# Attention weights staged in sixteen tiles, the key/query ring set up in the first plan, and the last query part stores issued by ScalarE

## The chip, the core and the metric

One core of a Trainium2 chip runs the whole program. Its compute engines are TensorE (PE in the profile, with its weight loads as PEld), VectorE (DVE), ScalarE (ACT) and GpSimd (POOL); SyncE (SP) issues DMAs. Each engine has one queue of instructions and takes them in order. An instruction that waits for another engine holds back everything behind it on its own queue. The metric is the device time of one execution in microseconds (us); lower is better. A time and the span of the profiled execution differ by what lies around the first and the last instruction.

## The reference

The program computes one decoder layer for 32 batches of 128 positions and 512 features, in float32. Cut to what matters:

```python
x = layernorm(x + attn(x))          # 16 heads; sequence of 128; causal; rotary
x = layernorm(x + xattn(x, ctx))    # 8 heads; here features attend to features
x = layernorm(x + ffn(x))           # 512 -> 2048 -> 512, quantized

def xattn(q, c):                     # per batch (128, 512), seen as 8 heads of 16 rows
    s = einsum('hdq,hdl->hql', q, c) / sqrt(16)      # 512 x 512 scores per head
    return gamma * einsum('hql,hdl->hdq', softmax(s), c)

def ffn(x):
    h = gelu(silu(bitlinear(x, w1, b1)))
    h = layer_norm(h) * ln_g + ln_b
    return bitlinear(h, w2, b2)      # rms norm, rounding to 8 bit, ternary weights
```

The attention's weights Wq, Wk, Wv and Wo are float32 and stay so; the feed-forward weights are rounded to -1, 0, 1.

## The kernel before, in words

The kernel has two stages, one after the other, with all 32 batches in each.

**Stage 1** (to about 560 us) does the self-attention. The four weight matrices are loaded in sixteen pieces of 128 x 512 (`split_weight`, `part`, lines 311 to 321). Each piece is split into a high part, which ScalarE or VectorE casts (lines 317 and 315), and a low part, which VectorE subtracts (line 318). A projection is then twelve matmuls (`project`, line 346): high by high, low by high, high by low. The pieces pass through a staging tile `wst` with four buffers, so the fifth load waits until the first piece is split. `load` (line 332) fetches a batch of x twice, turned (`xt`) and plain (`xs`). `stage_q` makes the projections and the rotary products, `stage_s` the scores, the masked softmax and its transposes, `stage_o` the weighted sum, the output projection and the first layernorm. Its result x1 is stored to DRAM (line 521). `split3` cuts it into three bfloat16 parts in a tile `sp`, and stores six part copies of 128 KB to `q_d` (line 364, from SP). `context` does the same for the context into `k_d`, and stores the values to `c_d` (line 381). All PSUM tiles of stage 1 come from one group of eight banks.

**Stage 2** does cross-attention and the feed-forward part. For each batch and each half of the heads, a key tile `kp` and a query tile `qp` are loaded from `k_d` and `q_d` (six parts of 16 rows, 96 rows). They live in a ring of four pairs (`NQ`). `b1_` makes 16 products (line 677), of which VectorE takes row maxima (line 681); `shift` turns the maxima on TensorE (line 691), splits them in two (lines 694, 695), and SP stores them as rows 96 and 97 of `qp` (line 700). `b2_` can then make the shifted scores (line 756), ScalarE their exponentials (line 759), and TensorE the sum with the values `cT` (line 766), whose upper half is ones, so that the denominators come along. `final`, `up_`, `gelu_` and `down_` make the second layernorm and the feed-forward part.

**The hand-over.** The ring lies where the weights of q, k and v were. When the last projection matmul of q, k, v has been put into the program, `early` (line 578) opens the ring and issues twelve loads from SP: the ones rows (line 587) and, for all four pairs, keys and queries (line 589). The value tiles `cT` belong to a pool of stage 2 and are opened and set to one by GpSimd (line 616) behind all of stage 1; the first load into them is line 663. The sixteen products of the first half batch belong to stage 2's plan.

**What sets the order.** Everything is emitted by a list planner (`Plan`, line 83), once per stage. Operations are filed under a kind such as `SP.xs` or `PE.mx`; within a kind they keep their order. At each step the planner takes, of the heads of all kinds, the one that can start first by its own cost figures; starts are compared in steps of `slack` microseconds, and within one step the lower priority number goes first. The priority is the batch number plus a figure for the kind (`OFF1`, `OFF2`). `rel` keeps an operation from starting before a planned time. On each engine the order so found is the order of the program; at run time an engine waits for what the order demands.

## Time and profile before

| what | value |
|---|---|
| median of 3 runs | 1673.24 us (1671.13 to 1677.36) |
| the profiled execution's own time | 1675.28 us |
| its span | 1673.5 us |
| mean granted TensorE clock | 0.973 of full speed |
| busy share of the span: TensorE, VectorE, ScalarE, GpSimd | 93%, 83%, 86%, 75% |
| last projection matmul of q, k, v in stage 1 ends | 549.12 us |
| last output projection matmul ends | about 562.6 us |
| first shifted score of stage 2 | 585.55 us |

The page gives the span in 40 slices of about 42 us each with the busy share of every engine in tenths. The windows view gives the same for stretches of one's own choice: length, then busy time of each engine with the number of its instructions, then the granted TensorE clock, the busy share of the DMA engines and GB/s. The timeline lists instructions by start, with length, engine, line and operand names; for the DMA queues a merged row stands for several issues. The waits view lists who waited for whom: total us, times, longest.

### The profile page before, as it was taken

What the parts mean: (1) busy time and instruction counts of PE and PEld (TensorE: products, weight loads), DVE (VectorE), ACT (ScalarE), POOL (GpSimd) and SP (SyncE); (2) the same over time, 40 slices, a digit from 0 to 9 for tenths busy, and PEclk for the clock granted to TensorE, in tenths of its full rate; (3) what the DMA queues carried; (4) which work ended last, traced back from release to release, by engine and by line L of the source; (5) the groups of instructions that cost most, each with busy time, mean ns of one, the idle gap of its engine ahead of it and who ended that gap; (6) DMA issues with size and microseconds to landing.
All of it is one profiled execution on the core that took longest, in us unless ns stands there. A gap on an engine that the chain in (4) does not pass through costs nothing.

```text
span 1673.5 us, 30270 instructions
## 1 busy us (share of the span) xinstructions
PE 1551.4 (93%) x9540; PEld 785.0 (47%) x9540; DVE 1383.9 (83%) x3315; ACT 1432.7 (86%) x2950; POOL 1251.5 (75%) x1679
## 2 busy tenths in 40 slices
PE   6999999999999799999999999999999999999844
PEld 4878777777778333333333333333333333333211
DVE  6877776777777678899999989899899999998674
ACT  4889989899976367999989989899999999998963
POOL 3777778777787404679879888878978888986772
PEclk8999999999999799999999999999999999999977
DMA  6476677766664654355455345545544544544221
GB/s 226 163 236 232 226 231 244 255 233 214 209 208 153 185 177 122 93 129 145 113 133 147 105 129 139 131 115 139 142 110 128 153 110 134 149 122 123 69 62 50
DMA packets 235680, 258.71 MB, mean 155 GB/s; under 512 B 110072, under 2 KB 159224, under 8 KB 235136
## 3 DMA queue, kind: packets, MB, share of 16 engines
q1 hardware_dynamic: 235520, 256.78, 52.8%
q8 instruction: 75, 1.23, 0.3%
q14 instruction: 85, 0.70, 0.1%
HBM read 142.41 MB, written 92.81 MB: 141 GB/s over the span
## 4 chain that ended last, share of the span: by engine, by line
PE 41%; DVE 18%; POOL 16%; DMA 9%; ACT 8%; issue 7%; SPq 1%; POOLq 0%; ACTq 0%; DVEq 0%
PE banka L346 12%; DVE mt L681 8%; PE acc L766 7%; PE sT L756 6%; POOL z L972 6%; PE mx L677 5%; PE m L925 2%; DVE am L998 2%; PE banka L477 2%; DMA qd<-sp 2%; POOL z L794 2%; PE banka L447 2%; ACT pr L465 1%; ACT ex L759 1%; PE banka L496 1%
## 5 line engine op out<-in xcount | busy, mean ns | idle before, releaser
L681 DVE TENSOR_REDUCE mt<-mx 128x1 f32<-128x512 f32 x1024 | 643.4, 679 | 54.9 <-PE mx L677 52.9
L759 ACT ACTIVATE ex<-sT 128x512 f32<-128x512 f32 x1024 | 533.9, 615 | 77.9 <-PE sT L756 74.4
L677 PE MATMUL mx<-kp,qp 96*128 96x512 bf16 x1024 | 336.9, 386 | 21.5 <-DVE mt L681 17.7
L756 PE MATMUL sT<-qp,kp 98*128 98x512 bf16 x1024 | 320.7, 385 | 15.9 <-DMA qp<-mlo 13.3
L766 PE MATMUL acc<-ex,cT 128*32 128x512 f32 x2048 | 289.4, 637 | 0.0
L465 ACT ACTIVATE pr<-pr,nm 128x128 f32<-128x128 f32 x512 | 198.9, 394 | 4.1 <-DVE nm L459 4.1
L756 PEld LDWEIGHTS <-kp 98*128 98x128 bf16 x1024 | 90.3, 98 | 223.7 <-issue 125.1
L677 PEld LDWEIGHTS <-qp 96*128 96x128 bf16 x1024 | 96.3, 98 | 195.5 <-issue 95.1
L972 POOL TENSOR_TENSOR z<-z,bb_b 128x512 f32<-128x512 f32 x119 | 154.4, 1301 | 0.3
L972 POOL TENSOR_TENSOR z<-z,g_b 128x512 f32<-128x512 f32 x119 | 153.5, 1297 | 0.5
L459 DVE CUSTOM_DVE_ANT_0 pr<-banka,cmask 128x128 f32<-128x128 f32 x512 | 111.0, 286 | 35.9 <-PE banka L447 35.2
L1009 PE MATMUL m<-w2q,q2T 128*128 128x512 fp8e4 x464 | 116.7, 385 | 16.4 <-DMA q2T<-q 16.4
L766 PEld LDWEIGHTS acc<-ex,cT 128*32 128x32 f32 x2048 | 70.6, 184 | 114.1 <-issue 108.8
L925 PE MATMUL m<-w1q,q1T 128*128 128x512 fp8e4 x464 | 119.1, 378 | 2.7 <-DVE z L928 1.3
L1009 PEld LDWEIGHTS <-q2T 128*128 128x128 f16 x512 | 51.0, 101 | 104.5 <-DMA q2T<-q 34.9
L465 ACT ACTIVATION_READ_ACCUMULATOR pr<-pr,nm 128x1 f32 x512 | 98.0, 191 | 0.0
L794 POOL TENSOR_SCALAR z<-z,nmu,rs 128x512 f32<-128x512 f32 x119 | 94.5, 801 | 1.8
L361 POOL TENSOR_TENSOR sp<-spr,sp 128x512 bf16<-128x512 f32 x64 | 76.7, 1200 | 20.3 <-ACT sp L359 18.2
L928 DVE SCALAR_TENSOR_TENSOR z<-m,dq,b_b 128x512 f32<-128x512 f32 x116 | 85.0, 733 | 1.8 <-PE m L925 1.5
L925 PEld LDWEIGHTS <-q1T 128*128 128x128 f16 x512 | 49.2, 97 | 76.1 <-issue 19.9
L846 POOL TENSOR_TENSOR num<-num,rden 128x512 f32<-128x512 f32 x29 | 37.1, 1278 | 62.3 <-DMA rden<-rd 62.2
L346 PE MATMUL banka<-wqkh,xh 128*128 128x512 f32 x256 | 73.9, 411 | 10.3 <-ACT xh L388 10.3
(152 smaller groups left out, 3247.9 us busy)
## 6 DMA issues: line engine op xcount, KB each, us to landing
kd<-sp SPq DMA_DIRECT2D x192, 128.0 KB
qd<-sp SPq DMA_DIRECT2D x192, 128.0 KB
kp<-kd SPq DMA_DIRECT2D x64, 384.0 KB
qp<-qd SPq DMA_DIRECT2D x64, 384.0 KB
F<-f SPq DMA_DIRECT2D x64, 256.0 KB
xt<-in_xT SPq DMA_DIRECT2D x32, 256.0 KB
xs<-in_x SPq DMA_DIRECT2D x32, 256.0 KB
ct<-in_cxT SPq DMA_DIRECT2D x32, 256.0 KB
```

The lines of the kernel that those rows point to most:

```text
L346: nc.tensor.matmul(pq.t, parts[a].t[:, c, :], w[t][:, c, sl], start=k == 0, stop=k == 11)
L459: nc.vector.tensor_tensor_reduce(pr.t[:, c, :], sc.t[:, c * P:(c + 1) * P], cmask, -1.0, 3e38, ALU.add, ALU.min, nm.t[:, c:c + 1])
L465: nc.scalar.activation(pr.t[:, c, :], pr.t[:, c, :], AF.Exp, scale=-1.0, bias=nm.t[:, c:c + 1], accum_out=den.t[:, c:c + 1])
L677: nc.tensor.matmul(sc.t[:, j, :], q.t[0:NPR, h, (qc + j) * P:(qc + j + 1) * P], k.t[0:NPR, h, :], start=True, stop=True)
L681: pl.op("DVE.mx", 0.064 + 0.534 * W, lambda: nc.vector.tensor_reduce(mt.t[:, i:i + W], sc.t, AX.X, ALU.max), (sc,), (mt,), p, join=True)
L756: nc.tensor.matmul(sc.t[:, i, :], k.t[:, h, lc * P:(lc + 1) * P], q.t[:, h, :], start=True, stop=True)
L759: pl.op("ACT.ex", 0.052 + 0.426 * SW, lambda: nc.scalar.activation(ex.t[:, j:j + SW, :], sc.t, AF.Exp, scale=1.0 / XD ** 0.5), (sc,), (ex, ...
L766: nc.tensor.matmul(acc.t[32 * h:32 * h + 32, :], v.t[:, :, XH * lc + 4 * g + h], exs[h // 2].t[:, h % 2, :], start=lc == 0, stop=lc == NC - 1)
L794: pl.op(e + "." + p, cost + 0.1, lambda: en(e).tensor_scalar(o.t[:, sl], v.t[:, sl], sh.t, sc.t, ALU.add, ALU.mult), ins, outs, prio)
L925: nc.tensor.matmul(flat(pz)[:, i * 512:(i + 1) * 512], q1T.t[:, c, :], w1q[:, c, (n + i) * 512:(n + i + 1) * 512], start=c == 0, stop=c == ...
L972: pl.op(e + kind, 0.148 + 0.0021 * w if e == "Pool" else 0.05 + 0.00105 * w, lambda: en(e).tensor_tensor(t(), t(), other[:, sl], op), src, ...
L1009: nc.tensor.matmul(flat(py)[:, 0:D], q2T.t[:, c, :], w2q[:, c, :], start=c == 0, stop=c == NI - 1)
```

## The change

Six things are changed.

- **Weights.** The sixteen weight pieces are staged in sixteen different tiles: seven of tag `prT`, five of `pr` and four of `wst`, all of which stage 1 has anyway. No weight load waits for an earlier piece. The low part of six of the sixteen pieces is made by GpSimd. The load of the first `xt` gets priority -1000.
- **Ring.** The value tiles `cT` are opened and set to one in `early`, beside the ring. `early` issues only the ones rows; the eight key and query loads become planned operations of stage 1 (`SP.kq`), held back until the stores they read and the last q, k, v matmul.
- **Carry.** The products, maxima and shift of the first half batch (`b1_` for batch 0, half 0) are planned in stage 1, in two PSUM banks of its group (`mx=2`).
- **Stores.** The six query part stores of each of the last two batches are issued by ScalarE (`ACT.xsd`).
- **Planner.** `op` takes extra dependencies (`after`); a projection matmul counts 0.244 us instead of 0.236; stage 1's `slack` is 0.05 instead of 0.02.
- **Figures.** Every figure in `OFF1` and `OFF2` is another, so the order is another in both stages.

The functions `b1_`, `shift`, `last`, `slow`, `eng`, `bank` and `flat` move ahead of stage 1 with the same arithmetic. The diff, cut (of the configuration and the planner's figures only a few entries are shown):

```diff
-CFG = dict(..., early=5, ...)
+CFG = dict(..., carry=1, ...)
-OFF2 = {'SP.const': -264.67, 'x.kq': 390.3, 'SP.v': 77.29, 'PE.mx': -381.13, 'DVE.mx': 126.92, ...}
+OFF2 = {'SP.const': -363.47, 'x.kq': 222.35, 'SP.v': 14.78, 'PE.mx': -501.79, 'DVE.mx': 339.36, ...}
-OFF1 = {'SP.x': 76.47, 'SP.w': -83.56, 'ACT.w': 1251.46, 'DVE.wl': 97.39, ..., 'SP.xs': 975.4}
+OFF1 = {'SP.x': 75.59, 'SP.w': -99.74, 'ACT.w': 1071.41, 'DVE.wl': -171.32, ..., 'SP.xs': 1284.61,
+  'ACT.xsd': 162.58, 'SP.kq': 326.77, 'PE.mx': 327.89, 'DVE.mx': -118.6, 'PE.mT': 188.75, ...}
-C1 = dict(pace=15.0, ..., tr=3, sc=4, ..., slack=0.02)
+C1 = dict(late=2, pace=15.0, ..., tr=3, mx=2, sc=4, ..., slack=0.05)
...
+        stage = ["prT"] * C1["prT"] + ["pr"] * C1["pr"] + ["wst"] * C1["wst"]
...
                 def part(c, sl=sl, w=w):
-                    t = pl.buf("wst")
-                    dma("w", lambda: nc.sync.dma_start(t.t, src[:, c, sl]), 262, (), (t,), -1.0)
+                    tag = stage.pop(0)
+                    t = pl.buf(tag)
...
+                    dma("w", lambda: nc.sync.dma_start(flat_(), src[:, c, sl]), 262, (), (t,), -1.0)
...
-                    pl.op("DVE.wl", 0.6, lambda: nc.vector.tensor_tensor(
-                        lo[:, c, sl], t.t, hi[:, c, sl].bitcast(F32), ALU.subtract), (t,), (w,), -1.0)
+                    e = "Pool" if c == 3 or c == 1 and name != "wqk" else "DVE"
+                    pl.op(e + ".wl", 0.6 if e == "DVE" else 1.23, lambda: en(e).tensor_tensor(
+                        lo[:, c, sl], flat_(), hi[:, c, sl].bitcast(F32), ALU.subtract), (t,), (w,), -1.0)
...
-            dma("x", lambda: nc.sync.dma_start(xt.t, xT[b]), 262, (), (xt,), at, (b - 1.5) * C1["pace"])
+            dma("x", lambda: nc.sync.dma_start(xt.t, xT[b]), 262, (), (xt,), at if b else -1000.0, (b - 1.5) * C1["pace"])
...
-                pl.op("PE." + kind, 0.236 * m, mm, used + [wb], (pq,), prio)
+                pl.op("PE." + kind, 0.244 * m, mm, used + [wb], (pq,), prio)
...
             for s, k in enumerate(parts):
-                dma(kind, lambda s=s, k=k: nc.sync.dma_start(dst[s].rearrange("t h c -> h t c"), sp.t[:, k, :]), 131,
-                    (sp,), (), prio)
+                q = nc.scalar if late else nc.sync
+                pl.op("ACT.xsd" if late else "SP." + kind, 0.55, lambda s=s, k=k, q=q: q.dma_start(
+                    dst[s].rearrange("t h c -> h t c"), sp.t[:, k, :]), (sp,), (), prio, 2.6)
...
-            split3("xs", x1, q_d[b], Q_PARTS, at)
+            split3("xs", x1, q_d[b], Q_PARTS, at, b >= NB1 - C1['late'])
...
+        for i in range(NQ):
+            b, g = divmod(i, 2)
+            K[b, g], Q[b, g] = pl.buf("kp"), pl.buf("qp")
+            for t, d, kind in ((K[b, g], k_d, "cs"), (Q[b, g], q_d, "xs")):
+                dma("kq", lambda t=t, d=d, b=b, g=g: nc.sync.dma_start(
+                    t.t[0:NPR], d[b][:, :, 4 * g:4 * g + 4, :].rearrange("s t h c -> (s t) h c")), 393, (), (t,), NB1 + b + 0.5 * g,
+                    after=pl.kinds["SP." + kind][6 * b:6 * b + 6] + pl.kinds["PE.qkv"][-1:])
+            if i < CARRY:
+                b1_(b, g, NB1 + b + 0.5 * g)
...
             qk = pool(ctx, "qk", side="right")
+            for i in range(CFG["cT"]):
+                t = qk.tile([P, 2 * XD, NC * XH], F32, tag=f"cT{i}", name=f"cT{i}")
+                nc.gpsimd.memset(t[:, XD:], 1.0)
+                vring.append(t)
             for i in range(NQ):
...
                 nc.sync.dma_start(k[NPR:NROW], ones_d)
-                for t, d in ((k, k_d), (q, q_d))[:2 if i < min(CFG['early'], NQ) else 0]:
-                    nc.sync.dma_start(t[0:NPR], d[i // 2][:, :, 4 * (i % 2):4 * (i % 2) + 4, :].rearrange(
-                        "s t h c -> (s t) h c"))
...
-    vring = [cb.tile([P, 2 * XD, NC * XH], F32, tag=f"cT{i}", name=f"cT{i}") for i in range(CFG["cT"])]
-    for t in vring:
-        nc.gpsimd.memset(t[:, XD:], 1.0)
...
         for g in range(2):
-            b1_(b, g)
+            if 2 * b + g >= CARRY:
+                b1_(b, g, b + 0.5 * g)
```

## Prediction

> **What bounds the kernel now.** I read the page first. TensorE is busy 93% of the span, and in the 40 slices only three places differ from full: the first slice, the fourteenth (in both the granted clock falls too), and the end. The change touches the first two.
>
> ```profile
> PE 1551.4 (93%) x9540; PEld 785.0 (47%) x9540; DVE 1383.9 (83%) x3315; ACT 1432.7 (86%) x2950; POOL 1251.5 (75%) x1679
> ...
> PE   6999999999999799999999999999999999999844
> ...
> PEclk8999999999999799999999999999999999999977
> ```
>
> Then the windows view around these two places. The start (three lines) gives TensorE nothing for 10.29 us, and then little at a low clock. The hand-over (two lines) gives it 27 instructions in 22.90 us, at a clock of 0.57, while ScalarE works 1.85 us.
>
> ```profile
> 0.00:10.29 10.29, 0.00 (x0) 0.00 (x0) 3.53 (x6) 3.14 (x4) 1.17 (x13) 1.00 0.71 236
> 10.29:19.23 8.94, 5.88 (x16) 4.24 (x16) 5.76 (x9) 3.58 (x5) 4.63 (x5) 1.00 0.82 260
> 19.23:33.80 14.57, 11.93 (x63) 9.01 (x61) 9.93 (x16) 4.51 (x8) 4.80 (x5) 0.65 0.54 161
> ...
> 549.00:562.60 13.60, 12.08 (x85) 9.11 (x84) 7.10 (x15) 9.47 (x33) 11.10 (x15) 1.00 0.90 228
> 562.60:585.50 22.90, 13.60 (x27) 2.39 (x25) 16.84 (x30) 1.85 (x3) 6.72 (x11) 0.57 0.56 189
> ```
>
> Why the start is slow: SP's own waits in the first 45 us. Weight loads (line 313) wait for the subtraction that empties their staging tile.
>
> ```profile
> SPq L313 <- DVE wvl L318: 5.2, 3, 3.4
> SPq L313 <- DVE wqkl L318: 4.6, 4, 2.1
> SPq L313 <- DVE wqkh L315: 3.2, 2, 2.0
> ```
>
> Why the hand-over is slow: SP's timeline there. 24 query part stores go out one after another, then the value load stands until the last of them has landed, and the shift rows (line 700), whose operands VectorE had ready at 574.87, stand behind it.
>
> ```profile
> 557.17 5.69 SPq L364 DMA_DIRECT2D qd<-sp  x6
> 563.31 1.27 SPq L521 DMA_DIRECT2D x1d<-x  x2
> 564.77 6.51 SPq L364 DMA_DIRECT2D qd<-sp  x10
> 571.42 0.38 SPq L521 DMA_DIRECT2D x1d<-x  x1
> 572.05 5.31 SPq L364 DMA_DIRECT2D qd<-sp  x8
> 582.37 0.33 SPq L663 DMA_DIRECT2D cT<-cd  x1
> 582.75 0.62 SPq L700 DMA_DIRECT2D qp<-mhi  x1
> ```
>
> The waits of that stretch say who pays: ScalarE 14.1 us for the first shifted score, GpSimd 9.1 us for the place of the value tiles.
>
> ```profile
> ACT ex L759 <- PE sT L756: 16.1, 5, 14.1
> ...
> POOL cT L616 <- DMA qd<-sp: 9.1, 1, 9.1
> ```
>
> **The parts. Start.** By 33.80 us TensorE has done the first batch's 36 projection matmuls, 8 transposes and 32 small score matmuls. At full clock these cost 36 x 0.233 (later the chain has 16 in 3.73 us) + 0.9 (0.44 per four) + 1.1 = 10.4 us, so 23.4 us are lost. After the change the `xt` load goes first. The first load of before, issued at 1.63, was cast at 4.54, so `xt` arrives at about 4.5. The DMA engines moved 314 to 359 GB/s between 4 and 12 us, so a 262 KB piece follows every 0.8 us: the first four by 7.8, the last cast (0.62) at 8.4. TensorE starts at about 8. The early matmuls took 1.91 us per four; with 18 of 36 at that rate and 18 at 0.233 the projections end at 8 + 8.6 + 4.2 = 20.8, and with transposes and scores the second batch could begin at 22.8: 11 us earlier, if nothing waits. But the rotary chain (VectorE 1.5 us, GpSimd 1.9 us, transposes, copy) still stands between products and scores, and casts of wv crowd it; I take half, 6 us. On the other side: the two GpSimd pieces ahead of a rotary sum cost 2 x 1.28 us (the GpSimd subtraction of `xl`), +2.6 us, and the second batch's `xt`, now behind sixteen pieces, lands at about 4.5 + 17 x 0.8 = 18 us, before it is needed. Six low parts off VectorE save 6 x 0.69 = 4.1 us there and cost GpSimd 6 x 1.28 = 7.7 us, which its waits for `xh` (15.2 us) and for the rotary products (10.1 us) hide; without that cover they delay each batch's sums. These are inside the 6.
>
> [...] The row first: the subtraction at 12.29 took 1.35 us beside GpSimd's `xl` (11.81 to 13.09), against 0.69 elsewhere. [...]
>
> **Hand-over.** Four things move at once.
>
> The value tiles: three memsets of 0.52 us leave the chain at 582.45 and come to 549, where GpSimd may wait for the last projection matmul and holds the `spr` subtraction behind it: at most 1.5 us on a queue that is busy 11.10 of 13.60 us. The value load then has no stores to wait for, and the shift rows of the first half batch are in stage 1's plan. With maxima as late as now, rows issued at 574.9 rather than 582.75 give the first score 7.8 us earlier, at 577.7.
>
> The carried products: the first of them waited at 563.43 for the last reader of stage 1's banks. In stage 1's own group they need only the first ring pair, 768 KB issued from 549.5, landing at about 555. VectorE needs 16 x 0.6 = 9.6 us for their maxima plus some 5 us of stage 1's own between 555 and 570, so they end at about 569.5, not 573.7: 4 us more, score at 573.5 (12 us earlier) at best.
>
> The stores: an issue takes 0.576 us on SP, and 24 of them with waits took 17.5 us, 0.73 each. Twelve go to ScalarE, 6.9 to 8.8 us, inside the 6.3 + 14.1 us for which ScalarE waited there; behind them on its queue stand the first exponentials. Without that cover they cost up to 8.8 us. SP, rid of them, can issue the x1 store of batch 29 earlier, so that GpSimd's last `x` (568.86, after 2.8 us of waiting for that store) moves to 566; the last parts are ready at 570.6, six ScalarE stores end at 574.2, and with the landing of 4.9 us (577.36 to 582.25) the last is down at 579. The eight ring loads stay where they are in time: on SP after 549, ahead of the last stores.
>
> What is late next: stage 2's exponential tiles lie over stage 1's tiles. The value tiles waited for the last store to land; if the exponentials must too, they start at 579.5 instead of 586.22, 6.7 us earlier. So the ends are 12 and 6.7 us if all goes well, and +1 if ScalarE's stores are bare; I take 8, near the lower good end, because the only row of such a wait is the value tiles'. A shorter hole also leaves less at half clock: from 585.9 to 588.1 products come every 0.43 us instead of 0.22; I count 1 us.
>
> [...] The row: while SP alone stored, from 572 to 577, the DMA engines were 0.62 busy at 219 GB/s, with one 128 KB store issued per 0.66 us (8 in 5.31). [...]
>
> **Order.** All planner figures differ, and so do `slack` and the projection cost. No instruction's length changes. Between 640 and 1600 us TensorE waited 14.1 us for maxima, 6.2 for shift rows and 6.5 for exponentials, and at the end 40 us for transposed activations. A third of the first three either way is 9 us, of the tail a tenth 4 us. I take zero: the rows name no direction.
>
> ```profile
> PE mx L677 <- DVE mt L681: 14.1, 34, 1.7
> PE sT L756 <- DMA qp<-mlo: 6.2, 6, 2.5
> ```
>
> **Sum.** 6 + 8 + 1 = 15 us. Between the two places TensorE is busy 98%, so what is gained at the start isn't given back. The profiled execution goes from 1673.5 us of span (1675.28 us in all) to 1658.5 (1660.3); it was 2.0 us above the median, so the median goes from 1673.24 to 1658.
>
> **The rivals.** *Both holes close almost wholly* (start 11, hand-over 12, clock 1 to 2): 1649. For it: nothing in the rows forbids it but the place of the exponentials; against: the rotary chain. *One of the two holds*: ScalarE's stores stall it, or the last store is no earlier (hand-over 1 to 3), or the rotary chain sets the start anyway (0 to 2): 1673 - 7 = 1666, at the edge of what can be told apart. For it: the DMA engines were 0.90 busy at 549 to 562.60, so the stores may be late through bytes, not issues. *The new order costs more than the holes give*: in stage 2 the scores wait for the shift rows once per batch, because SP's queue puts other loads ahead. Now that is 6 waits of about 1 us in 31 batches; at 1 us in each, 31 us, the time is 1673 - 15 + 31 = 1689. It makes the kernel slower beyond 0.5% from 0.75 us per batch (15 + 8.4 over 31). For it: the longest such wait is 2.5 us. Against: SP's queue has room.
>
> **How the numbers follow.** The forecast 0.50, with a range of its own of 1650 to 1666; both holes closed 0.18; one holds 0.18; the order costs 0.14. What a measurement of this kernel can tell from no change is about 0.5%, 8.4 us: below 1664.9 is faster. The forecast gives 0.48 of its 0.50 to faster, the second case 0.18, the third falls within: faster 0.66, same 0.20, slower 0.14. The range runs from 1644 (start 11, hand-over 12, and a little from the order) to 1676 (one holds, and the order's 9 us against it); about 0.07 lies below it and 0.12 above.
>
> **What would show it.** First TensorE matmul at about 8 us and the second batch's projections before 29; no SP wait of line 313 on line 318; the ten low parts left on VectorE at 0.69 us. First shifted score between 573 and 579, ScalarE's wait before its first exponential under 8 us, no wait of the value tiles on query stores, and a clock above 0.6 in the hand-over. The distance from the first shifted score to the end, 1673.5 - 585.55 = 1088 us, stays. The prediction is wrong if that distance moves by more than 9 us, or if ScalarE's first exponential still waits for a landing query store after 582.

## The result and the profile after

The changed kernel is slower: 1691.20 us median of four runs (1686.67 to 1695.26) against 1672.26 us for the kernel before (four runs), a ratio of 1.0107 with an interval of 1.0073 to 1.0140. I had forecast 1658, within 1644 to 1676.

The profiled execution took 1686.67 us, the lowest of its four. It shows a span of 1684.9 us where before it was 1673.5; so the traces can account for 11.4 us of the 18.9 between the medians, and distances read from one execution carry a few microseconds of doubt. The verdicts of the experiments rest on the ratios, the places on the traces.

The page of the changed kernel, busy shares and the 40 slices of TensorE and of its clock:

```profile
PE 1552.0 (92%) x9540; PEld 782.5 (46%) x9540; DVE 1381.8 (82%) x3309; ACT 1430.1 (85%) x2950; POOL 1254.3 (74%) x1685
...
PE   7999999999999599999999999999999999999844
...
PEclk9999999999999899999999999999999999999977
```

The first slice is fuller (7 for 6), the fourteenth emptier (5 for 7): the hand-over now takes a larger part of TensorE's time in that slice, not a smaller one. The windows view of the same places, three lines for the start and two for the hand-over (length, then busy time of TensorE, weight loads, VectorE, ScalarE, GpSimd with instructions, then clock, DMA share, GB/s):

```profile
0.00:6.06 6.06, 0.00 (x1) 0.01 (x1) 0.02 (x1) 2.52 (x3) 2.09 (x14) 1.00 0.56 159
6.06:14.00 7.94, 5.00 (x10) 3.12 (x11) 6.48 (x10) 3.53 (x5) 2.46 (x3) 1.00 1.03 351
14.00:24.70 10.70, 8.54 (x33) 6.58 (x32) 10.70 (x16) 3.15 (x6) 9.17 (x8) 0.84 0.84 310
...
555.00:569.30 14.30, 12.80 (x89) 8.72 (x88) 10.78 (x22) 9.31 (x32) 10.52 (x17) 1.00 0.70 181
569.30:588.50 19.20, 2.38 (x12) 0.82 (x10) 7.48 (x15) 1.23 (x2) 5.04 (x7) 0.62 0.64 209
```

The start does what it was meant to do: first product at 6.06 instead of 10.29, second batch's projections at 24.7 instead of 33.8. But the last output projection ends at 569.3, where before it was 562.6: what looks like a lead of 9 us has become a lag of 7. The hole behind it is 19.2 us instead of 22.9, and 12 instructions stand in it instead of 27. The first shifted score comes at 588.5 instead of 585.5, and from there to the end it takes 1096.4 us instead of 1088.0. So three stretches are to be explained:

| stretch, one profiled execution each | before | after |
|---|---|---|
| to the second batch's projections | 33.8 | 24.7 |
| from there to the end of the last output projection | 528.8 | 544.6 |
| from there to the first shifted score | 22.9 | 19.2 |
| from there to the end | 1088.0 | 1096.4 |

The first two rows need care. When the second batch begins, the changed kernel has 40 matmuls behind it and the kernel before 76: four transposes and the 32 small score matmuls of the first batch come later in the new order. Seven of the sixteen carried products also stand before the end of the last output projection now. So some of the 15.8 us by which the second row grows is work that has changed sides.

What holds up the hand-over shows in SP's queue of the changed kernel (start, length from first to last issue of the row, line, transfer):

```profile
569.38 5.00 SPq L601 DMA_DIRECT2D x1d<-x  x2
574.48 3.94 SPq L444 DMA_DIRECT2D qd<-sp  x6
578.52 0.41 SPq L601 DMA_DIRECT2D x1d<-x  x1
579.97 0.33 SPq L745 DMA_DIRECT2D cT<-cd  x1
583.74 0.62 SPq L314 DMA_DIRECT2D qp<-mhi  x1
584.71 0.56 SPq L314 DMA_DIRECT2D qp<-mlo  x1
```

VectorE has the parts of the shift at 577.33; the rows go out at 583.74. SP's waits from 557 to 590, and ScalarE's wait at the end of it:

```profile
SPq L601 <- DMA kp<-kd: 6.8, 1, 6.8
SPq L601 <- DMA qd<-sp: 4.3, 1, 4.3
SPq L314 <- DMA x1d<-x: 3.4, 1, 3.4
...
ACT ex L782 <- PE sT L779: 13.7, 7, 11.0
```

These are odd waits. The store of x1 (line 601) does not read what a ring load (`kp<-kd`) writes, nor what a query store (`qd<-sp`) reads; the shift rows have nothing to do with the store of x1. The traces explain them: they give every transfer the counter on which its landing is told. In the kernel before, SP's 1275 transfers have eight counters strictly in turn. In the changed kernel SP's 1263 leave out twelve places of that turn, and ScalarE's twelve stores have just these, in the same order. The three late issues, each with the transfer that had its counter before (times in us):

| SP issues | at | the counter's transfer before it | issued at | landed at |
|---|---|---|---|---|
| store of x1 | 569.38 | ring load `kp<-kd`, SP | 559.93 | 569.32 |
| store of x1 | 574.05 | query store `qd<-sp`, ScalarE | 568.50 | 573.98 |
| shift rows `qp<-mhi` | 583.74 | store of x1, SP | 578.52 | 583.68 |

In each of the three the issue comes 0.06 to 0.07 us after that landing. So with stores on ScalarE, SP is not rid of them: here it stood 4.3 us behind one of them when the turn came round.

In stage 1, the waits of TensorE from 34 to 160 us in the changed kernel:

```profile
PE banka L557 <- DVE pr L550: 2.3, 4, 0.7
PE banka L576 <- ACT prT L560: 1.6, 2, 1.5
PE banka L557 <- DVE rd L548: 1.3, 2, 0.8
PE banka L557 <- POOL pr L550: 0.4, 1, 0.4
```

and in the kernel before:

```profile
PE banka L496 <- ACT prT L480: 0.6, 1, 0.6
PE banka L477 <- DVE pr L470: 0.5, 2, 0.3
PE banka L477 <- ACT pr L465: 0.4, 1, 0.4
```

5.6 us against 1.5: the transposes (line 557, before 477) and the weighted sums (576, before 496) are put into the program at places where the probabilities are not ready yet. This is a fault of the order, not of the engines. The windows view of 80 to 160 us says the same: TensorE is busy 74.36 us in the changed kernel and 79.02 in the kernel before.

### The profile page after: what moved, and what is told of

The parts are those of the page before. It is cut to its first block, busy times and chain, and to the rows that moved or that the text cites. A ratio compares the mean times of both kernels' runs of the same rounds, so it can differ in the third digit from the quotient of the medians.

```text
span 1684.9 us, 30306 instructions
## 1 busy us (share of the span) xinstructions
PE 1552.0 (92%) x9540; PEld 782.5 (46%) x9540; DVE 1381.8 (82%) x3309; ACT 1430.1 (85%) x2950; POOL 1254.3 (74%) x1685
## 4 chain that ended last, share of the span: by engine, by line
PE 31%; POOL 17%; DVE 14%; DMA 12%; ACT 12%; issue 4%; SPq 2%; POOLq 0%; ACTq 0%; DVEq 0%
PE banka L425 7%; DVE mt L294 6%; PE acc L789 6%; PE sT L779 6%; POOL z L995 5%; PE mx L290 5%; DMA rden<-rd 3%; ACT ex L782 2%; ACT pr L545 2%; PE m L948 2%; PE banka L557 2%; POOL z L817 2%; PE m L1032 1%; DMA den<-F 1%; DVE am L1021 1%
## 5 line engine op out<-in xcount | busy, mean ns | idle before, releaser
L294 DVE TENSOR_REDUCE mt<-mx 128x1 f32<-128x512 f32 x1008 | 632.0, 676 | 50.4 <-PE mx L290 48.8
L290 PE MATMUL mx<-kp,qp 96*128 96x512 bf16 x1008 | 330.3, 383 | 22.0 <-DVE mt L294 15.5
L779 PE MATMUL sT<-qp,kp 98*128 98x512 bf16 x1024 | 323.5, 387 | 22.9 <-DMA qp<-mlo 12.3
L557 PE MATMUL banka<-ident,pr 128*128 128x128 f32 x512 | 76.5, 276 | 12.3 <-DVE pr L550 5.6
L831 POOL TENSOR_SCALAR rsa<-mv 128x1 f32<-128x1 f32 x64 | 12.6, 197 | 99.9 <-DVE mv L825 78.8
```

The source lines that it names most:

```text
L290: nc.tensor.matmul(flat(sc)[:, j * D:(j + 1) * D], q.t[0:NPR, h, (qc + j) * P:(qc + j + 1) * P], k.t[0:NPR, h, :], start=True, stop=True)
L294: pl.op("DVE.mx", 0.064 + 0.534 * W, lambda: nc.vector.tensor_reduce(mt.t[:, i:i + W], flat(sc).rearrange("p (a b) -> p a b", a=W), AX.X, ...
L779: nc.tensor.matmul(sc.t[:, i, :], k.t[:, h, lc * P:(lc + 1) * P], q.t[:, h, :], start=True, stop=True)
```

## The experiments

Two theories. **O**: the new parts are worth about what they seemed, and the newly planned order gives it back. **P**: the parts can't be worth it, since stage 1 runs at the pace of something else, or the parts cost by themselves. Beside them the question what the stores on ScalarE do. All kernels here compute everything. The kernel before had a median of 1674 to 1676 us on the chips of the experiments; each ratio is against the kernel before on the same chip.

### New parts, old figures

```diff
-OFF1, OFF2 of the changed kernel; slack=0.05; "PE." + kind, 0.244 * m
+OFF1, OFF2 of the kernel before;  slack=0.02; "PE." + kind, 0.236 * m
```

> The changed kernel with the planner's figures of the kernel before (priorities of both stages, step 0.02, projection cost 0.236); the new kinds keep the changed kernel's figures. Theory A, the new figures cost the time: the parts alone keep their gains (the second batch starts about 9 us earlier, and the middle of stage 1 gives nothing back), so the last output projection ends near 554 us and the time is 1655 to 1665. Rival B, the parts themselves break the order of stage 1 and the hand-over, whatever the figures: the last output projection ends after 562 us and the time is 1680 or more.

Measured: 1696.32, ratio 1.0117 (1.0078 to 1.0156). The second batch's projections start at 23.6, the last q, k, v product ends at 547.9, but the last output projection only at 580.0, and the end comes 1112.8 us after the first shifted score. Old offsets on new parts make a new order, and a bad one. This did not separate O from P.

### Old parts, new figures

```diff
-OFF1, OFF2 of the kernel before;       slack=0.02; "PE." + kind, 0.236 * m
+OFF1, OFF2 of the changed kernel;      slack=0.05; "PE." + kind, 0.244 * m
```

> The kernel before with the changed kernel's figures (priorities, step 0.05, projection cost 0.244) and none of its parts. Theory A, the figures: slower, stage 1 longer by 8 to 16 us and stage 2 by up to 8, 1685 to 1697. Rival B, the parts: within 5 us of the kernel before, 1668 to 1677.

Measured: 1693.27, ratio 1.0103 (1.0061 to 1.0145). Without any new part, the new figures alone cost as much as the whole change. From the second batch's projections to the last output projection it took 548.5 us (528.8 before). For O.

### The late stores back on SP

```diff
-C1 = dict(late=2, ...)
+C1 = dict(late=0, ...)
```

> The changed kernel with all query part stores issued by SP (late=0). Theory C, eight completion counters taken in turn tie SP's issues to ScalarE's stores: SP's waits for landing query stores go, the x1 stores of the last batches go out earlier, the first shifted score comes 4 to 8 us earlier after the last output projection (now 19.3 us after it), and the time falls by as much, 1683 to 1687. Rival D, the stores are late through bytes or through GpSimd's chain, and SP is merely the issuer: that distance stays at 19 us or grows by the 7 us of twelve issues, 1691 to 1698.

Measured: 1686.96, ratio 1.0061 (1.0042 to 1.0080); from the last output projection to the first shifted score 11.6 us instead of 19.2, and from there to the end 1103.5 instead of 1096.4. So the stores on ScalarE cost time (1.0107 with them). The planner orders anew here too; TensorE's matmuls came out in the same order, but the kernels with a held order below are the cleaner test.

### The value tiles early, alone

```diff
         def early():
             st2.close()
             qk = pool(ctx, "qk", side="right")
+            for i in range(CFG["cT"]):
+                t = qk.tile([P, 2 * XD, NC * XH], F32, tag=f"cT{i}", name=f"cT{i}")
+                nc.gpsimd.memset(t[:, XD:], 1.0)
+                vring.append(t)
...
-    vring = [cb.tile([P, 2 * XD, NC * XH], F32, tag=f"cT{i}", name=f"cT{i}") for i in range(CFG["cT"])]
-    for t in vring:
-        nc.gpsimd.memset(t[:, XD:], 1.0)
```

> The kernel before with one edit: the value tiles are opened and set to one beside the ring, early. The planner knows nothing of it, so the order is the same to the last instruction but for three memsets. Theory E, the value load that waited for the last store's landing was what held the shift rows: it goes out near 577.5, the shift rows at 578 to 580 (their counters were last used by stores issued near 573), the first shifted score 3 to 5 us earlier, time 1668 to 1670. Rival F, stage 2's tiles wait for the same landing anyway: the first exponential stays at 586 us and the time at 1672.

Measured: 1674.79, ratio 0.9988 (0.9966 to 1.0010). The wait of the value load for the last store's landing is gone: it goes out at 579.39, right behind the last store, and the first shift rows at 580.19, where before they were at 582.37 and 582.75. From the last output projection to the first shifted score it takes 20.1 us instead of 22.9. Of these 2.8 us the time shows about 1, which is not apart from nothing, so E's 1668 to 1670 is missed.

### Holding the order

The next kernels don't let the planner choose. The order in which it emitted the operations of a kernel was recorded (a list of kinds; within a kind the order is fixed), and the planner takes, of the heads that can start, the one that comes first in a given list:

```diff
-                    key = (int(t / self.slack), o.prio)
+                    key = rank[k, i] if order else (int(t / self.slack), o.prio)
...
-        end = pl.run({"PE.qkv": early})
+        end = pl.run({"PE.qkv": early}, unpack(*ORDER1))
...
-    end = pl.run()
+    end = pl.run((), unpack(*ORDER2))
```

**The start alone, held.** The kernel before with the sixteen staging tiles, GpSimd's six low parts and the first load ahead:

```diff
-                    t = pl.buf("wst")
+                    tag = stage.pop(0)
+                    t = pl.buf(tag)
...
-                    pl.op("DVE.wl", 0.6, ...
+                    e = "Pool" if c == 3 or c == 1 and name != "wqk" else "DVE"
+                    pl.op(e + ".wl", 0.6 if e == "DVE" else 1.23, ...
...
-            dma("x", ..., (xt,), at, (b - 1.5) * C1["pace"])
+            dma("x", ..., (xt,), at if b else -1000.0, (b - 1.5) * C1["pace"])
```

> The kernel before with the sixteen staging tiles, the six low parts on GpSimd and the first input load ahead of the weights. The planner doesn't choose here: the order up to the last weight operation is the changed kernel's recorded one, and from there on all that is left goes in the recorded order of the kernel before, the whole of stage 2 with it. Theory O (the parts are worth what they seem and the newly planned order gives it back): the second batch's query projection starts 8 to 10 us earlier, the last projection ends 5 to 9 us earlier, and the time is 5 to 9 us below that of the kernel before (about 1664 to 1667 where before is 1672). Rival P (a lead of nine microseconds can't be held, whatever the order, because stage 1 runs at the pace of something else): the lead at the second batch is the same, it is gone by the last projection, and the time is within 3 us of the kernel before.

Measured: 1672.75 where before is 1675.93, ratio 0.9984 (0.9966 to 1.0003). The second batch's projections start at 23.4; the last output projection ends at 557.6, 5.0 us earlier than in the kernel before; the first shifted score comes at 580.6 and the end 1088.8 later. That reads like a lead of 10 us at the second batch of which 5 are left at the end of stage 1. But two other kernels run TensorE's matmuls of stage 1 in the very order of the kernel before, and their marks differ:

| one profiled execution each | second batch's projections | last matmul of the first output projection starts | last output projection ends |
|---|---|---|---|
| before | 33.8 | 70.3 | 562.6 |
| value tiles early (above) | 31.2 | 67.7 | 564.3 |
| late stores on ScalarE, held (below) | 30.8 | 67.3 | 561.3 |
| start alone, held | 23.4 | 63.8 | 557.6 |

So single executions of one order lie 3 us apart, and the 33.8 of the kernel before is the slowest of three. And the first mark compares unlike work (40 matmuls done against 76). From the first output projection on, the kernels have done the same matmuls at the same mark: there the lead is 3.5 to 6.5 us, and at the end of stage 1 it is 3.7 to 6.7. What the start gained, 4 to 7 us, was kept; the time shows 3 us of it, not safely apart from nothing.

**Everything, held.** The changed kernel with `ORDER1` and `ORDER2` as the expectation says.

> The whole changed kernel, but in recorded orders: its own up to the last weight operation, then that of the kernel before for the rest of stage 1 (the ring loads, the sixteen carried maxima and their shift rows stand behind the operation that they follow in the changed kernel), and that of the kernel before for stage 2. Theory O: the start's 5 to 9 us are kept, the hand-over gives between nothing and 5, stage 2 runs at the length of before (first shifted score to the end 1086 to 1091 us): 1658 to 1668. Rival P, or the operations themselves cost the time: first shifted score to the end stays at 1094 or over, or stage 1 is as long as in the changed kernel: 1678 or over.

Measured: 1675.23, ratio 0.9997 (0.9981 to 1.0012). This is the main result. The same parts as the changed kernel, the same transfers, carried maxima and stores on ScalarE; only the order is another, and the loss of 1.1% is gone. From the second batch's projections to the last output projection it took 537.0 us (544.6 in the changed kernel), from the first shifted score to the end 1090.7 (1096.4). P as I had put it (1678 or over) falls. But O's 1658 to 1668 is missed too: the gain that was forecast isn't there, and it ends where the kernel before does.

**Late stores on ScalarE, held.** The kernel before, with its whole order, and

```diff
-            split3("xs", x1, q_d[b], Q_PARTS, at)
+            split3("xs", x1, q_d[b], Q_PARTS, at, nc.scalar if b >= NB1 - 2 else nc.sync)
```

> The kernel before in its recorded order, and only the last two batches' query stores, six each, issued by ScalarE at the places in the program where SP issued them. Theory L (SP's and ScalarE's transfers share eight completion counters in the order of the program, so that SP waits behind ScalarE's stores): first shifted score 3 to 8 us later than in the kernel before, 1675 to 1681. Rival G (the prediction's: SP rid of the issues sends the hidden states' stores and the shift rows earlier): first shifted score 2 to 8 us earlier, 1664 to 1670.

Measured: 1680.21, ratio 1.0026 (1.0008 to 1.0044). From the last output projection to the first shifted score 28.2 us instead of 22.9. SP's waits in this kernel from 555 to 595 (line 724 loads the values, line 425 stores query parts):

```profile
SPq L724 <- DMA qd<-sp: 9.2, 4, 7.1
SPq L425 <- DMA qd<-sp: 6.6, 4, 4.9
```

In the kernel before the value load waits less, and the stores wait only for ring loads, not for one another:

```profile
SPq L663 <- DMA qd<-sp: 4.8, 4, 2.8
...
SPq L364 <- DMA qp<-qd: 1.9, 2, 1.0
```

SP's queue does not move on earlier with twelve issues fewer; it stands longer, and the shift rows go out at 586.71 where before it was 582.75.

**Everything, held, and all stores on SP.** One word against the kernel with everything held:

```diff
-                q = nc.scalar if late else nc.sync
+                q = nc.sync
```

> The kernel with everything held, and the twelve late query stores issued by SP at the same places in the program. Theory L (ScalarE's stores hold SP through the shared completion counters): last output projection to the first shifted score 3 to 9 us shorter than the 20.9 of the kernel with everything held, and the time 3 to 8 us below it and below the kernel before (1667 to 1672 where before is 1675). Rival: the twelve issues hold SP itself for as long as the counters did, and the time is within 2 us of the kernel with everything held.

Measured: 1669.53, ratio 0.9972 (0.9953 to 0.9990), against 0.9997 with the stores on ScalarE. From the last output projection to the first shifted score 14.8 us instead of 20.9. SP's queue in this kernel (line 375 sends the shift rows, 505 the query parts, 806 loads the values):

```profile
567.52 1.34 SPq L505 DMA_DIRECT2D qd<-sp  x2
568.96 0.62 SPq L375 DMA_DIRECT2D qp<-mhi  x1
569.68 0.56 SPq L375 DMA_DIRECT2D qp<-mlo  x1
570.33 3.88 SPq L505 DMA_DIRECT2D qd<-sp  x6
574.26 0.47 SPq L806 DMA_DIRECT2D cT<-cd  x1
```

The shift rows go out as soon as the maxima are there, ahead of the last six stores. Against the kernel with the start alone (23.1 us), the hand-over is 8.3 us shorter. But the end comes 1093.2 us after the first shifted score instead of 1088.8, and the times differ little: 3.2 us by the medians, 2 by the ratios, each measured on another chip. What took the rest shows in ScalarE's timeline, first in the kernel with the start alone (score at 580.6), then in this one (score at 574.1):

```profile
581.32 1.57 ACT L829 ACTIVATE ex<-sT 128x512 f32<-128x512 f32 x3 [14.11 <-PE sT L826]
```

```profile
577.94 3.21 ACT L843 ACTIVATE ex<-sT 128x512 f32<-128x512 f32 x6 [10.89 <-DMA cT<-cd]
```

The first exponential starts only 3.4 us earlier; counted from the last output projection, 18.6 us after it instead of 23.8. It no longer waits for the score; it waits for a transfer to land, 3.8 us beyond the score. The row names the load of the values, which the exponentials don't read. The landings in the trace say otherwise: ScalarE's wait ends at 577.73, when the last query store, issued at 573.65, has landed (577.71); the value load lands only at 578.36. In the last kernel below the same wait, 9.6 us, is put down to a query store (`qd<-sp`) by the view itself. It fits the tiles of the exponentials lying over those of stage 1.

### Which order costs

One stage held at a time, the other in the changed kernel's own order:

```diff
-        end = pl.run({"PE.qkv": early}, unpack(*ORDER1))
+        end = pl.run({"PE.qkv": early})
     end = pl.run((), unpack(*ORDER2))
```

> The changed kernel with its own order of stage 1, and with stage 2 in the recorded order of the kernel before (without the sixteen maxima, the transpose and the shift rows that the change carries into stage 1). If the order of stage 2 costs its part: first shifted score to the end 1088 to 1092 us where the changed kernel had 1096.4, first shifted score unchanged (586 to 590), some 5 to 8 us below the changed kernel and still 5 to 12 over the kernel before. Rival (stage 2 is longer because fewer maxima are done when it begins, whatever its order): first shifted score to the end 1094 or over.

Measured: 1677.96, ratio 1.0031 (1.0008 to 1.0054); 545.5 us from the second batch's projections to the last output projection, and 1088.7 from the first shifted score to the end. The stretches are as expected; the time is 2 us over the kernel before, where 5 to 12 were expected.

```diff
         end = pl.run({"PE.qkv": early}, unpack(*ORDER1))
-    end = pl.run((), unpack(*ORDER2))
+    end = pl.run()
```

> The changed kernel with stage 1 in the recorded order of the kernel before, as in the kernel with everything held, and with stage 2 in its own planned order. If the two orders cost separately: first shifted score at 579 to 584, first shifted score to the end 1094 to 1098, 2 to 7 us over the kernel before. Rival (stage 1's order is what costs, and stage 2 only runs on with the disorder that it was handed): first shifted score to the end 1088 to 1092, within 3 us of the kernel before.

Measured: 1683.20, ratio 1.0034 (1.0020 to 1.0048); 533.1 us and 1100.1 us in the same two stretches, the second a little over the 1094 to 1098 expected. (The kernel with everything held runs the same stage 1 and took 537.0: again one order, 4 us apart.)

Each stage's order costs by itself, where that stage is, whatever the other does: stage 1 some 8 to 12 us of its length, stage 2 some 8 to 9 of its own. In the times each alone costs 0.3 to 0.4% over the kernel with everything held; together, as in the changed kernel, 1.1%, so the times of the two don't simply add, and four runs of the changed kernel don't say more.

**Where stage 1 loses.** The kernel with everything held, but with the changed kernel's order up to the eleventh batch's projections instead of about 35 us (another `ORDER1`). In the trace TensorE leaves that order at 183 us, later than the 155 that I had expected:

```diff
-ORDER1: own order up to the last weight operation, then that of before
+ORDER1: own order up to the eleventh batch's projections, then that of before
```

> As the kernel with everything held, but the changed kernel's own order of stage 1 reaches up to the eleventh batch's projections (about 155 us), and only the rest is in the order of the kernel before. If stage 1 loses its microseconds in that stretch, where TensorE's transposes wait for the probabilities: the second batch's projection to the last output projection takes 541 us or more (537.0 with everything held, 544.6 in the changed kernel), and the time is 4 to 7 us above that of the kernel with everything held. Rival (the loss is spread over the stage): 538 to 540 us, within 3 us of it.

Measured: 1679.79, ratio 1.0030 (1.0014 to 1.0046); 542.9 us from the second batch's projections to the last output projection (537.0 with everything held). So 5.9 of the 7.6 us that the changed kernel is longer there are lost by 183 us; with 4 us between executions of one order, that says most of it, not an exact share. The stretch from 80 to 160 us, windows view, in this kernel

```profile
80.00:160.00 80.00, 74.34 (x616) 58.50 (x614) 55.10 (x228) 69.64 (x218) 61.22 (x71) 1.00 0.71 233
```

and with everything held

```profile
80.00:160.00 80.00, 78.97 (x667) 63.71 (x666) 58.55 (x254) 74.70 (x243) 63.29 (x74) 1.00 0.71 235
```

TensorE gets through 616 instructions instead of 667, at the same full clock; the changed kernel has the same 616. The waits of the transposes for the probabilities, shown above for 34 to 160 us, fall in this part of the stage.

**Where stage 2 loses.** In the kernels with the held order 25 maxima (16 of the first half batch, 9 of the second) are taken before the first shifted score; in the changed kernel 16. I meant to move the nine:

```diff
-ORDER2: the changed kernel's own
+ORDER2: the changed kernel's own, with PE.mx, DVE.mx nine times ahead of the first PE.sT
```

> Stage 1 in the recorded order of the kernel before, stage 2 in the changed kernel's own order with one change: the first nine maxima of the second half batch (products and reductions) stand ahead of the first shifted score, as they do in the kernel before; 25 maxima are then done when it starts, not 16. If that is what stage 2 lost: first shifted score to the end 1088 to 1093 us where the same kernel without the nine had 1100.1, and 5 to 9 us less in all. Rival (the rest of stage 2's order costs it): the distance falls by less than 3 us and the time stays 2 to 7 us over the kernel before.

Measured: 1687.05, ratio 1.0066 (1.0041 to 1.0091), 1100.3 us from the first shifted score to the end. But in the kernel the nine do not stand ahead. The list has them first, yet the planner took one score before them, and TensorE's timeline shows it:

```profile
578.07 0.58 PE L841 MATMUL sT<-qp,kp 98*128 98x512 bf16 x1 [12.32 <-DMA qp<-mlo]
578.45 4.99 PE L352 MATMUL mx<-kp,qp 96*128 96x512 bf16 x9
```

So 16 maxima were done when the first shifted score started, as in the changed kernel, and this run does not decide the question. One of the next two does in part.

Then stage 2 was split at the first shifted score of the 29th batch, one part in each order:

```diff
-ORDER2: one order throughout
+ORDER2: up to PE.sT number 896 one order, from there the other
```

> Stage 1 in the recorded order of the kernel before; stage 2 in the changed kernel's own order up to the first shifted score of the 29th batch, and from there on in the order of the kernel before. If stage 2 loses its microseconds over its length (TensorE busy some 10 us longer for the same products): first shifted score to the end 1096 us or more, as the 1100.1 with the own order throughout. Rival (they are lost in the last four batches): 1089 to 1093 us, within 3 us of the kernel with everything held.

> The other half of it: stage 1, and stage 2 up to the first shifted score of the 29th batch, in the order of the kernel before, and the last four batches in the changed kernel's own order. If stage 2 loses over its length: 1089 to 1093 us from the first shifted score to the end. Rival (the last four batches): 1096 us or more, 6 to 10 us over the kernel with everything held.

Measured: own order in the body 1678.86, ratio 1.0023 (1.0007 to 1.0039), 1098.5 us; own order in the last four batches 1682.85, ratio 1.0041 (1.0022 to 1.0061), 1100.9 us. The kernel with the own order in the last four batches alone has 25 maxima done before its first shifted score and is as long as the kernel with the own order throughout; so the missing nine maxima can't be all of it. Either half of the new order costs about as much as the whole. I can't name one place in stage 2 and leave it open; the joint of two orders may cost by itself.

### Another order, nothing else

> The kernel before with one figure of the planner changed: the slack of stage 1 0.05 in place of 0.02; every operation, tile and engine stays. Theory O (the offsets fit one order and its neighbours are worse, so any newly chosen order of stage 1 costs microseconds): 5 to 20 us slower than before, 1677 to 1692. Rival S (the planner's choice hardly matters, it is the new parts and the new offsets that cost): within 3 us of before.

```diff
-C1 = dict(..., wl=24.0, slack=0.02)
+C1 = dict(..., wl=24.0, slack=0.05)
```

Measured: 1669.74 where before is 1675.93, ratio 0.9962 (0.9942 to 0.9983). This goes against both expectations: one figure moved, no part changed, and the kernel is faster. O as I had put it, that the order of before is fitted and its neighbours are worse, is wrong. The orders newly planned here lie between 0.4% below and 1.2% above, and which way is not to be seen from the figures. The gain doesn't show in stage 1, whose order was changed: its last output projection ends at 562.1, as in the three kernels with the old order (561.3 to 564.3). The first shifted score follows 20.4 us later instead of 22.9, and the end 1086.5 after that instead of 1088.0.

### What does well, together

The start's parts on that order of stage 1 (`ORDER1` recorded from the kernel with slack 0.05, spliced behind the start as above):

> The start's parts alone, spliced as in the kernel with only the start held, but on the order of stage 1 that the planner makes for the kernel before with its slack at 0.05; stage 2 in the recorded order of the kernel before. If order and start add up: 8 to 11 us below the kernel before (the 3 of the held start and the 6 of that order). Rival (both take up the same idle time of TensorE): no faster than the better of the two, 4 to 7 us below the kernel before.

Measured: 1668.45, ratio 0.9955 (0.9937 to 0.9973); first shifted score at 577.3. By the medians that is 7.3 us below the kernel before, between the two ranges; by the ratio it is not apart from that order alone (0.9962). So adding up is not shown, though the profiled execution, with a span of 1663.5, is the first below 1665.

And with the value tiles and ring early, the maxima carried, and all stores on SP:

> What did well, together: the start's parts, the value tiles and the ring loads early, the sixteen maxima carried, all stores on SP, stage 1 in the order that the planner makes for the kernel before at a slack of 0.05, and stage 2 in the recorded order of the kernel before. If the parts add up: 9 to 14 us below the kernel before (0.9917 to 0.9946). Rival (the earlier first shifted score is given back behind it, as between the two kernels with more and less held): no better than start and that order alone, 5 to 8 us below.

Measured: 1664.05 where before is 1674.59, ratio 0.9941 (0.9921 to 0.9961), 10.5 us by the medians. The page, the hand-over (its second part, windows view) and ScalarE's wait from 565 to 634 in this kernel:

```profile
PE 1544.8 (93%) x9540; PEld 781.8 (47%) x9540; DVE 1383.4 (83%) x3309; ACT 1431.5 (86%) x2950; POOL 1261.5 (76%) x1685
...
PE   6999999999999799999999999999999999999844
```

```profile
557.50:570.70 13.20, 7.08 (x21) 1.85 (x19) 11.61 (x21) 1.24 (x2) 4.29 (x7) 0.68 0.57 199
```

```profile
ACT ex L843 <- DMA qd<-sp: 9.6, 1, 9.6
```

The hole is 13.2 us (22.9 before, 19.2 in the changed kernel), the first shifted score at 570.7 (585.5 and 588.5). The first exponential, held by the landing store, starts at 574.27. It beats both kernels, by 0.6% against the kernel before. Not all of that is the parts: the order of stage 1 without any part gave 0.9962, and the intervals of the two overlap. In the old order the same parts, stores on SP, gave 0.9972. So by these two the parts are good for some 0.2 to 0.3%, and the rest goes to the order.

| kernel | ratio to before | second batch to last output projection | to first shifted score | to the end |
|---|---|---|---|---|
| before | 1 | 528.8 | 22.9 | 1088.0 |
| changed | 1.0107 | 544.6 | 19.2 | 1096.4 |
| start alone, held | 0.9984 | 534.2 | 23.1 | 1088.8 |
| everything, held | 0.9997 | 537.0 | 20.9 | 1090.7 |
| the same, stores on SP | 0.9972 | 536.3 | 14.8 | 1093.2 |
| stage 2 held | 1.0031 | 545.5 | 18.7 | 1088.7 |
| stage 1 held | 1.0034 | 533.1 | 20.8 | 1100.1 |
| stores on ScalarE alone, held | 1.0026 | 530.5 | 28.2 | 1089.3 |
| slack 0.05 alone | 0.9962 | 530.9 | 20.4 | 1086.5 |
| all good parts | 0.9941 | 534.0 | 13.2 | 1092.2 |

The distances are from one execution each, and the same order differs by 3 to 4 us in them. The last column becomes clearer when it is counted from the first exponential instead of the first shifted score: all the kernels with stage 2 in the order of before then take 1085.5 to 1091.0 us to the end, those with the changed kernel's order, whole or in part, 1095.8 to 1100.3. (The first two experiments have yet other orders of stage 2 and take 1100.6 and 1092.5.)

## Why the prediction was wrong

Between the forecast ratio (1658 to 1673, 0.991) and the measured 1.0107 lie 2.0%, some 33 us. The new order is 1.1% of it (1.0107 against 0.9997 with the order held), the stores on ScalarE about 0.25% (0.9997 against 0.9972), and the remaining 0.6% is what the other parts gave less than the 15 us of the sum.

**Start, 6 us: the mechanism and the size right.** The first product came at 6.06 (8 forecast), the second batch's projections at 24.7 (before 29 forecast, and 22.8 if nothing waited; four transposes and 32 scores of the first batch were still to come). In the held order 4 to 7 us of lead show on the traces, up to the end of stage 1. No weight load waits for a subtraction any more. The low parts on VectorE did not take the 0.69 us that I had asked for: six of `wqkl` in the first 34 us

```profile
L400 DVE TENSOR_TENSOR wqkl<-prT,wqkh 128x512 fp32r<-128x512 f32 x6 | 5.2, 890 | 7.5 <-ACT wqkh L398 7.4
```

took 0.89 us each, and GpSimd's 1.31 to 1.48 us instead of 1.28. All ten took 9.6 us; at the mean of before in the first 34 us (11.9 us for 15) the sixteen would have taken 12.7, so six pieces moved to GpSimd saved VectorE about 3.1 us, not 4.1. (At the 0.69 us of an undisturbed one the ten would have taken 6.9.) A subtraction that began at 16.24 beside one of GpSimd (16.17 to 17.49) took 1.80 us; those at 10.11 and 13.71, while GpSimd stood idle, took 0.69 and 0.68.

The sentence of the sum, "Between the two places TensorE is busy 98%, so what is gained at the start isn't given back", holds as long as the order is held. It failed in the changed kernel, because the 98% belonged to the old order, and the change replaced that order: from 80 to 160 us TensorE was busy 79.02 us before and 74.36 after. The last output projection ended at 569.3 us, 9 to 13 us later than in the six kernels with the new parts and the held order of stage 1 (556.4 to 560.3).

**Hand-over, 8 us: right in sign for the early tiles and carried maxima together, wrong in sign for ScalarE's stores.** With the order held and all stores on SP, the first shifted score came 8.3 us sooner after the last output projection. The first step that failed is "SP, rid of them, can issue the x1 store of batch 29 earlier": SP waits for ScalarE's stores through the counters, and the twelve stores cost 5.3 us of hand-over and 0.26% of the time alone, 6.1 us and about 0.25% in the changed structure. In these two pairs of kernels twelve issues fewer on SP saved nothing, and time was lost. "The eight ring loads stay where they are in time" failed too: they went out from 558.18 to 562.20, before from 549.5, since they stand behind a last projection that ends 8 us later. ScalarE's wait before the first exponential was 11.0 us (below 8 forecast). In the changed kernel this wait was for the score alone, so the bound that I had put on the hand-over, that the exponentials may have to wait for the last query store to land, was not reached there. In the kernels with the shorter hole it was, and the term, 8 us, was mis-sized by it: after the last output projection the score came 8.3 us sooner, the first exponential 5.1, and from the first exponential on the length was that of before within the spread (1089.4 us, before 1087.3).

"The distance from the first shifted score to the end ... stays" failed for two causes: the order of stage 2 in the changed kernel (1096.4), and, with that order held, this wait (1093.2).

**Order, 0 us: the step that made the prediction wrong.** "I take zero: the rows name no direction." The rows did name none, but a bound of 9 us on stage 2's waits and 4 on its end left out stage 1 altogether, where the order alone is worth 8 to 12 us of length, most of it by 183 us. Holding the order took the whole loss of 1.1% away; new figures without new parts made 1.0103; and a nudge of one figure made 0.9962. By these runs the right entry was a range from some 6 us below to some 20 above, wider than all other terms together.

**The rivals.** "The new order costs more than the holes give" named the winner, at 1689 for 1691, but not its mechanism: TensorE's waits for the shift rows in stage 2 of the changed kernel are

```profile
PE sT L779 <- DMA qp<-mlo: 12.3, 2, 11.8
```

two waits, one of them the first score's, where I had priced one per batch. Its chance of 0.14 was far too small for a change in which every figure of the order was another.

## What to carry to other kernels

When a change re-plans the order, hold the order and run the parts on it before judging them: here that alone moved the result from 1.1% slower to even, and the parts that did well could then be told from the one that did not. A newly found order is a cost of its own, here from 0.4% below to 1.2% above; put that spread into the range, for every stage that is planned anew, also one where the bounding engine has little idle time. Of a gain at a hand-over, here 5.1 of 8.3 us reached the next engine: price the wait that stands next. And read a lead at a mark only where both kernels have done the same work, and against more than one execution: here one order gave marks 3 to 4 us apart.

## What the runs showed of the hardware that was not expected

Moving transfers from SP's queue to ScalarE's did not take them out of SP's way. In the trace of the changed kernel the 1275 transfers of both queues have eight counters in one common turn, and three late issues of SP waited for the landing of the transfer that had the same counter before, from either engine and unrelated to them: 6.8 us of the store of x1 for a ring load, 4.3 for a store by ScalarE, 3.4 of the shift rows for the store of x1. Twelve stores moved, in an otherwise equal program, made it 4.3 us slower by the medians (1680.21 against 1675.93).
